# Layer 1's attention in two parts a group: products and copies behind the group's maximum, VectorE's use of them at the group's end, and x added two tiles at a time

## The chip, the cores and the metric

The kernel runs on one core of one Trainium2 chip. The metric is the device time of one execution in microseconds (us), the median of several runs. A separate execution, taken with the hardware profiler, gives the profile and the trace.

## What is computed

The program is a graph network of two layers on 3125 nodes of 256 features, float32 throughout. The part that matters here is the middle of layer 1, which takes the normalised x and adds two things to x: an attention over 50000 edges, and a linear attention over all nodes ("Galerkin").

```python
xn = _layernorm(x)
x = x + _L1_gnn_ref(xn, edge_index, ...) + _L1_mix_ref(xn[None], Wqkv, Wout, bout)[0]

# edges: a message per edge, softmax weights per head, sums per target node
messages = h_fwd[src] * direction[:, 0:1] + h_rev[src] * direction[:, 1:2]
scores = leaky_relu(einsum('ef,hf->eh', messages, attn_forward[0]), 0.2)
exp_scores = exp(scores - scores.max(axis=0))
norm = exp_scores / (segment_sum(exp_scores, dst)[dst] + 1e-10)
out[h] = segment_sum(messages * norm[:, h], dst)

# Galerkin: 8 heads of 64; k and v are normalised over the head
q, k, v = split(xn @ Wqkv.T)
k, v = inst_norm(k), inst_norm(v)
dots = einsum('bhnd,bhne->bhde', k, v)
out = (q @ dots / n) @ Wout.T + bout
```

## The kernel before, in words

`layer0_ffn` ends with 14 adds of x and rows read back from DRAM (L915), two for each of seven chunks of tiles (a tile is 125 nodes; CHUNKS has four of 4 tiles and three of 3). `layer1_mix` then normalises x (`layernorm`, L168 to L185), which leaves the transposed xT, and multiplies each tile by the weights of the edge messages (L191 with wcat). The rows go to a table in DRAM (tab1). Outside the blocks named below, a scheduler decides each engine's order when the program is built.

The loop over edges is written out by hand: in `manual_schedule` the orders of TensorE (PE), VectorE (DVE) and ScalarE (ACT) are those of the program text. The 391 columns of 128 edges are walked in 49 groups of 8. GpSimd (POOL) gathers the rows of a group, three groups ahead, into one of four buffers (`fetch`, L51). A group i then does the following:

- `messages` (L1221 to L1230): DVE forms the messages and the scores of group i and their maximum per partition; PE transposes that (L1232).
- `weigh` (L1278): DVE multiplies the messages of group i - 1 by their weights.
- `maximum` (L1239 to L1241): DVE reduces the transposed maximum, and PE brings the new and the old maximum back to all partitions (L1245).
- `products` (L1286): PE sums the weighted messages of group i - 1 into nodes, with one-hot matrices, in PSUM tiles pw.
- `add` (L1295, L1297): DVE rescales and adds the sums of group i - 2; ACT copies some (L1300, L1302).
- `ones_of` (L1270): DVE builds the one-hot matrices of group i.
- `exponents` (L1250 to L1255): DVE subtracts the maximum, ACT takes Exp.
- `next(todo)`: one step of the generator `galerkin`.

`galerkin` is cut into steps by its `yield`s, and the loop takes one step at the end of each group. Group 0 loads and transposes the weights of k and v (L1456) and takes the mean out of them (L1461 to L1463). Groups 1 to 26 run its loop over 25 tiles: the step first uses tile t - 1 (DVE reduces its squares, L1472, ACT takes Sqrt, L1476, DVE scales v, L1477 and L1478, PE adds to dots, L1480), then makes tile t (PE multiplies xT by the weights, L191, ACT copies the two halves, L1490, and squares them, L1492). Group 27 takes dots out of PSUM and transposes Wout, group 28 forms m2 (L1512, L1513), group 29 forms gm (L1521, L1523). Groups 29 to 35 add the result to x, a chunk each: for each tile PE multiplies xT by gm (L191) into one of the two buffers of the PSUM pool ps_a, and DVE adds it to x (L1529); one more DVE instruction adds bout to the chunk (L1530). Groups 36 to 48 have no step left.

After the loop DVE divides by the sums and adds the edges' result to x. `layer1_ffn` follows and is the same in both kernels.

Of the kernel before, what the change touches and what calls it, by code (L numbers as in the profile page):

```python
# [8 lines left out]
F32 = mybir.dt.float32  # L9
# [79 lines left out]
class Kernel:  # L89
# [1078 lines left out]
    def layer1_mix(self):  # L1168
        nc, tc, a = self.nc, self.tc, self.a
        W, HD = 68, 64  # L1170
        with ExitStack() as m:
# [134 lines left out]
            with tc.manual_schedule(engines={E_.PE, E_.DVE, E_.Activation}):  # L1306
                todo = self.galerkin(big, wk, ps_a, ps_c, xT)
                starts = [(j0, min(GROUP, NJ - j0)) for j0 in range(0, NJ, GROUP)]
                G = len(starts)
                ahead = [fetch(starts[i][0]) for i in range(3)]  # L1310
                msg, exps, summed = {}, {}, {}
                for i in range(G + 2):
                    if i + 3 < G:
                        ahead.append(fetch(starts[i + 3][0]))
                    if i < G:
                        j0, n, g = ahead[i]
                        o, s, pt = messages(j0, n, g)
                    if 0 <= i - 1 < G:
                        weigh(starts[i - 1][1], msg[i - 1][0], exps[i - 1][2])
                    if i < G:  # L1320
                        pb = maximum(pt)
                    if 0 <= i - 1 < G:
                        summed[i - 1] = products(*starts[i - 1], exps[i - 1][2], msg[i - 1][1])
                    if 0 <= i - 2 < G:
                        add(*starts[i - 2], *exps[i - 2][:2], summed[i - 2])
                    if i < G:
                        msg[i] = o, ones_of(j0, n)
                        exps[i] = exponents(n, s, pb)
                    next(todo, None)
                last = exps[G - 1][0]  # L1330
# [112 lines left out]
    def galerkin(self, big, wk, ps_a, ps_c, xT):  # L1443
# [5 lines left out]
        for c4 in range(2):  # L1449
# [3 lines left out]
            for k in range(2):  # L1453
                pt = ps_a.tile([128, 4, 128], F32, name="ln_pt")
                for i in range(4):
                    nc.tensor.transpose(pt[:, i, :], nat[:, i, k * 128:(k + 1) * 128], self.ident)  # L1456
                nc.scalar.copy(wkv[:, k, 512 * c4:512 * c4 + 512],
                               pt.rearrange("p a b -> p (a b)"))
        heads = wkv.rearrange("p k (h c) -> p (k h) c", c=64)
        mean = big.tile([128, 32], F32, name="wkv_mean")  # L1460
        nc.vector.tensor_reduce(mean, heads, AX.X, OP.add)  # L1461
# [4 lines left out]
        pc = ps_c.tile([128, 4, 128], F32, name="pdots")  # L1466
        kvs = {}
        for t in range(NT + 1):
            if t > 0:
                kv, sq = kvs.pop(t - 1)  # L1470
                var = wk.tile([P, 16], F32, name="kv_var")
# [7 lines left out]
                for hp in range(4):  # L1479
# [2 lines left out]
                                     kv[:, 2 * hp:2 * hp + 2, :].rearrange("p a b -> p (a b)"),  # L1482
                                     start=(t == 1 and hp == 0), stop=(t == NT and hp == 3),
                                     skip_group_check=True)
            if t < NT:
                kv = wk.tile([P, 16, 64], F32, name="kv")
                for i in range(2):
                    pk = ps_a.tile([P, 512], F32, name="ln_pt")
                    self.token_matmul(pk, xT, t, wkv[:, :, 512 * i:512 * i + 512])
                    nc.scalar.copy(kv[:, 8 * i:8 * i + 8, :].rearrange("p a b -> p (a b)"), pk)  # L1490
                sq = wk.tile([P, 16, 64], F32, name="kv_sq", bufs=1)
                nc.scalar.activation(sq, kv, AF.Square)  # L1492
                kvs[t] = kv, sq
            yield
        dots = big.tile([128, 4, 128], F32, name="dots")
        nc.vector.memset(dots, 0.0)
        for s in (slice(0, 64), slice(64, 128)):
            nc.vector.tensor_copy(dots[s, :, s], pc[s, :, s])

        woT = big.tile([128, 4, D], F32, name="woT")  # L1500
        nat = wk.tile([128, 2, 512], F32, name="nat4", bufs=1)
        nc.sync.dma_start(nat, a["L1_mix_Wout"].rearrange("(c p) f -> p c f", p=128))
        for cc in range(2):
            pt = ps_a.tile([128, 4, 128], F32, name="ln_pt")
            for i in range(4):
                nc.tensor.transpose(pt[:, i, :], nat[:, cc, i * 128:(i + 1) * 128], self.ident)
            nc.scalar.copy(woT[:, :, cc * 128:(cc + 1) * 128], pt)
        yield
        m2 = big.tile([128, 4, D], F32, name="m2")
        for hp in range(4):  # L1510
            pm = ps_a.tile([128, D], F32, name="ln_pt")
            nc.tensor.matmul(pm, dots[:, hp, :], woT[:, hp, :], start=True, stop=True)  # L1512
            nc.vector.tensor_scalar(m2[:, hp, :], pm, 1.0 / N, None, op0=OP.mult)  # L1513
        wq = wk.tile([128, 4, D], F32, name="nat4", bufs=1)
        nc.sync.dma_start(wq, a["L1_mix_Wqkv"][0:512, :].rearrange("(c p) d -> p c d", p=128))
        yield
        g = big.tile([128, 2, D], F32, name="gm")
        for k in range(2):
            pm = ps_a.tile([128, D], F32, name="ln_pt")
            for hp in range(4):  # L1520
                nc.tensor.matmul(pm, wq[:, hp, k * 128:(k + 1) * 128], m2[:, hp, :],  # L1521
                                 start=(hp == 0), stop=(hp == 3))
            nc.scalar.copy(g[:, k, :], pm)  # L1523
        bout = self.bcast(big, "L1_mix_bout")
        for t0, n in CHUNKS:
            for t in range(t0, t0 + n):
                pm = ps_a.tile([P, D], F32, name="ln_pt")
                self.token_matmul(pm, xT, t, g)
                nc.vector.tensor_add(self.x[:, t, :], self.x[:, t, :], pm)  # L1529
            nc.vector.tensor_add(self.x[:, t0:t0 + n, :], self.x[:, t0:t0 + n, :],  # L1530
                                 bout[:, None, :].to_broadcast([P, n, D]))
            yield


# [393 lines left out]
```

## Time and profile before

| what | value |
|---|---|
| runs shown: median (lowest to highest) | 2810.51 us (2807.82 to 2812.39), 3 runs |
| profiled execution | 3210.01 us, its span 3208.3 us |
| granted TensorE clock, mean over the span | 0.844 |
| busy over the span | PE 2295.1, DVE 1516.4, POOL 1640.0, ACT 539.8 us |
| first gather of the edge loop to the last maximum | 1865.4 to 2515.3 us |

The profile gives times of one execution from the start of its span. A line of the order of time has the start, the duration, the engine, the line of the source, the operation with "output<-inputs", the shapes, a count, and in brackets the idle time of the engine ahead of it with what ended it. "PEld" are PE's weight loads. A float32 matmul shows as two records ("x8" for four matmuls of L191). PEclk is the TensorE clock that was granted, as a share of full speed.

### The profile page before, as it was taken

The numbers are of one execution on the slowest core, as the hardware profiler recorded it, in microseconds if no ns is written. First come the engines' busy times: TensorE is split into PE (matmuls) and PEld (weight loads), VectorE is DVE, ScalarE is ACT, GpSimd is POOL, SyncE is SP. The second block draws the span as 40 slices with busy tenths as digits, with TensorE's granted clock in tenths as the row PEclk, the third lists the DMA queues.
The fourth block names the chain that finished last, engine by engine and source line by source line (L and its number), as shares of the span: only waits on it lengthen the run. The fifth ranks groups of instructions, "written<-read, shape, count | busy, mean of one in ns | idle before, by whom it ended". The sixth has DMA issues, their size and how long they took to land. (4 is left out here: it accounts for less than half of the span.)

```text
span 3208.3 us, 26947 instructions
## 1 busy us (share of the span) xinstructions
PE 2295.1 (72%) x9183; PEld 1705.1 (53%) x9183; DVE 1516.4 (47%) x3630; ACT 539.8 (17%) x1107; POOL 1640.0 (51%) x1490
## 2 busy tenths in 40 slices
PE   1753652169998699899999458798668564788773
PEld 1442431057675466788787345465546353555552
DVE  7874750065547760122111448688569810122225
ACT  1420000000000111222222124344000110122213
POOL 5887887700000170566666157777547246555612
PEclk9865765579998699999999779899878777989886
DMA  8904200034330020655554422221112210111133
GB/s 311 367 2 112 68 12 1 0 78 98 79 98 29 17 76 1 211 169 184 180 177 150 100 69 49 45 48 44 40 31 46 68 37 7 21 33 43 41 90 72
DMA packets 179585, 265.05 MB, mean 83 GB/s; under 512 B 54288, under 2 KB 143866, under 8 KB 176051
## 3 DMA queue, kind: packets, MB, share of 16 engines
q1 hardware_dynamic: 121057, 206.38, 21.1%
q0 software_dynamic: 52480, 47.70, 7.2%
q10 hardware_dynamic: 5894, 9.09, 0.8%
q8 instruction: 76, 1.25, 0.2%
q14 instruction: 78, 0.63, 0.1%
HBM read 178.73 MB, written 84.21 MB: 82 GB/s over the span
## 5 line engine op out<-in xcount | busy, mean ns | idle before, releaser
L51 POOL DMA_INDIRECT g<-tab,t_src x391 | 454.4, 1162 | 259.1 <-issue 111.4
L58 POOL DMA_INDIRECT adj<-ch_sum,ch_place x391 | 488.8, 1250 | 148.0 <-issue 119.4
L460 PE MATMUL psum<-sup,adjT 125*125 125x256 f32 x1250 | 328.2, 411 | 218.6 <-issue 164.5
L460 PEld LDWEIGHTS psum<-sup,adjT 125*125 125x125 f32 x1250 | 250.8, 203 | 285.2 <-issue 200.6
L58 POOL DMA_INDIRECT sorted<-s_rows,pos x256 | 245.9, 961 | 187.6 <-DVE s_rows L1055 119.1
L51 POOL DMA_INDIRECT G<-tabg,g_src x256 | 251.2, 981 | 159.5 <-DVE g_src L1613 83.9
L1286 PE MATMUL pw<-v,hot 128*125 128x260 f32 x1244 | 328.4, 427 | 0.0
L1286 PEld LDWEIGHTS pw<-v,hot 128*125 128x125 f32 x1244 | 259.0, 212 | 50.5
L1644 PE MATMUL fpy<-fw,fh 128*125 128x256 f32 x800 | 208.5, 418 | 86.8 <-ACT fh L1638 36.9
L864 PE MATMUL ph<-xs,w 128*128 128x256 f32 x1024 | 232.3, 385 | 33.4 <-issue 29.6
L1644 PEld LDWEIGHTS fpy<-fw,fh 128*125 128x125 f32 x800 | 164.5, 209 | 135.9 <-ACT fh L1638 43.4
L864 PEld LDWEIGHTS ph<-xs,w 128*128 128x128 f32 x1024 | 194.2, 192 | 71.3 <-issue 44.0
L892 PE MATMUL py<-w,h 128*128 128x256 f32 x1024 | 231.2, 379 | 0.0
L463 DVE TENSOR_TENSOR x<-x,psum 125x512 f32<-125x512 f32 (+1 forms) x104 | 69.1, 666 | 327.2 <-remote 169.4
L1636 PE MATMUL fph<-xT,fw 128*128 128x500 f32 (+1 forms) x448 | 181.2, 553 | 37.0 <-ACT fh L1638 34.0
L892 PEld LDWEIGHTS py<-w,h 128*128 128x128 f32 x1024 | 192.1, 190 | 24.8
L620 POOL MEMSET tier<- 125x64 f32 x1 | 0.2, 157 | 378.1 <-PE psum L460 378.1
L866 ACT ACTIVATE h<-ph,b 128x256 f32<-128x256 f32 x256 | 121.2, 474 | 392.4 <-PE ph L864 357.4
L1030 PE MATMUL pctx<-s_mv,s_ro 128*128 128x256 f32 x512 | 154.9, 413 | 1.9 <-DVE s_mv L1029 1.9
L1636 PEld LDWEIGHTS fph<-xT,fw 128*128 128x128 f32 x448 | 86.2, 195 | 111.8 <-issue 52.8
L170 ACT ACTIVATE ln_rs<-ln_mv,eps 125x4 f32<-125x4 f32 (+1 forms) x28 | 7.5, 296 | 793.0 <-DVE ln_mv L169 793.0
L1638 ACT ACTIVATE fh<-fph,cols 128x500 f32<-128x500 f32 (+1 forms) x112 | 69.5, 633 | 420.4 <-PE fph L1636 226.5
(524 smaller groups left out, 3435.7 us busy)
## 6 DMA issues: line engine op xcount, KB each, us to landing
adjT<-adj SPq DMA_DIRECT2D x25, 1367.2 KB
adj<-zero SPq DMA_DIRECT2D x22, 1536.0 KB
w<-in_L_ffn_W1p_dram SPq DMA_DIRECT2D x32, 1024.0 KB
w<-in_L_ffn_W2p_dram SPq DMA_DIRECT2D x32, 1024.0 KB
slots<-empty SPq DMA_DIRECT2D x1, 8448.0 KB
srow<-slots SPq DMA_DIRECT2D x32, 264.0 KB
adj<-ch_sum,ch_place POOLq DMA_INDIRECT x391
g<-tab,t_src POOLq DMA_INDIRECT x391
```

The lines of the kernel that those rows point to most:

```text
L51: nc.gpsimd.indirect_dma_start(out=out, out_offset=None, in_=table, in_offset=bass.IndirectOffsetOnAxis(ap=idx, axis=0))
L58: return nc.gpsimd.indirect_dma_start(out=table, out_offset=bass.IndirectOffsetOnAxis(ap=idx, axis=0), in_=rows, in_offset=None, **kw)
L460: nc.tensor.matmul(pm[:, i, :], mats[b][:, (a0 + i) * P:(a0 + i + 1) * P], sup[:, b, :], start=(b == b0), stop=(b == b0 + n - 1))
L463: nc.vector.tensor_add(xs, xs, pm[:, :m, :])
L864: nc.tensor.matmul(ph, w1[:, k, f * 128:(f + 1) * 128], xs[:, k, :], start=(k == 0), stop=(k == 1))
L866: nc.scalar.activation(h[:, f, :], ph, AF.Gelu, bias=b1[:, f:f + 1])
L892: nc.tensor.matmul(py, h[:, f, i * 128:(i + 1) * 128], w2[:, f, :], start=(f == 0), stop=(f == FC - 1))
L1030: nc.tensor.matmul(p1, ro[:, f - f0, :], mv, **st)
L1286: nc.tensor.matmul(pw.rearrange("p h c -> p (h c)"), hot[:, i - i0, :], v[:, i, :, :].rearrange("p h c -> p (h c)"), start=(i == i0), stop ...
L1636: nc.tensor.matmul(ph[:, :n * P], w1[:, k, f * 128:(f + 1) * 128], xT[:, k, t0 * P:(t0 + n) * P], start=(k == 0), stop=(k == 1))
L1638: nc.scalar.activation(hs[:, f, :n * P], ph[:, :n * P], AF.Gelu, bias=self.col("L1_ffn_b1", ei * FC + f))
L1644: nc.tensor.matmul(py, hs[:, f, i * P:(i + 1) * P], w2[:, f, :], start=(f == 0), stop=(f == FC - 1))
```

## The change

`galerkin` gets more `yield`s, and each group takes two steps instead of one. The new one stands behind the maximum of the group, ahead of the products of the edges; the old one stays at the end. The first step of a group holds what PE and ACT do for a tile (products, copies, squares), the second what DVE does with the tile before. The transposes of Wout, the products for m2 and gm and the products for x go into first steps, their uses into second ones. Further edits: the squares get two buffers instead of one; Wq is loaded ahead into a buffer of its own; the four products of m2 share two PSUM tiles, the two of gm one; two tiles of x share one PSUM tile and one add; bout is no longer added by VectorE but by a third matmul for each tile, of a row of ones with the row bout, and is loaded as one row. Since `galerkin` now has one step pair more ahead of the chunks, x is added in groups 30 to 36.

The orders of the built programs differ in two further places that the text doesn't touch. On DVE the 14 adds of L915 stood one after the other ahead of layernorm; now layernorm's instructions for a chunk stand between the adds of the next ones, and ACT's square roots and copies of layernorm follow chunk by chunk. On SP the load of Wq stands right behind the first load of the weights of k and v. The order on POOL is the same.

```diff
--- before.py
+++ after.py
@@ -1319,6 +1319,7 @@
                         weigh(starts[i - 1][1], msg[i - 1][0], exps[i - 1][2])
                     if i < G:
                         pb = maximum(pt)
+                    next(todo, None)
                     if 0 <= i - 1 < G:
                         summed[i - 1] = products(*starts[i - 1], exps[i - 1][2], msg[i - 1][1])
                     if 0 <= i - 2 < G:
@@ -1456,6 +1457,7 @@
                     nc.tensor.transpose(pt[:, i, :], nat[:, i, k * 128:(k + 1) * 128], self.ident)
                 nc.scalar.copy(wkv[:, k, 512 * c4:512 * c4 + 512],
                                pt.rearrange("p a b -> p (a b)"))
+        yield
         heads = wkv.rearrange("p k (h c) -> p (k h) c", c=64)
         mean = big.tile([128, 32], F32, name="wkv_mean")
         nc.vector.tensor_reduce(mean, heads, AX.X, OP.add)
@@ -1466,6 +1468,16 @@
         pc = ps_c.tile([128, 4, 128], F32, name="pdots")
         kvs = {}
         for t in range(NT + 1):
+            if t < NT:
+                kv = wk.tile([P, 16, 64], F32, name="kv")
+                for i in range(2):
+                    pk = ps_a.tile([P, 512], F32, name="ln_pt")
+                    self.token_matmul(pk, xT, t, wkv[:, :, 512 * i:512 * i + 512])
+                    nc.scalar.copy(kv[:, 8 * i:8 * i + 8, :].rearrange("p a b -> p (a b)"), pk)
+                sq = wk.tile([P, 16, 64], F32, name="kv_sq")
+                nc.scalar.activation(sq, kv, AF.Square)
+                kvs[t] = kv, sq
+            yield
             if t > 0:
                 kv, sq = kvs.pop(t - 1)
                 var = wk.tile([P, 16], F32, name="kv_var")
@@ -1482,21 +1494,7 @@
                                      kv[:, 2 * hp:2 * hp + 2, :].rearrange("p a b -> p (a b)"),
                                      start=(t == 1 and hp == 0), stop=(t == NT and hp == 3),
                                      skip_group_check=True)
-            if t < NT:
-                kv = wk.tile([P, 16, 64], F32, name="kv")
-                for i in range(2):
-                    pk = ps_a.tile([P, 512], F32, name="ln_pt")
-                    self.token_matmul(pk, xT, t, wkv[:, :, 512 * i:512 * i + 512])
-                    nc.scalar.copy(kv[:, 8 * i:8 * i + 8, :].rearrange("p a b -> p (a b)"), pk)
-                sq = wk.tile([P, 16, 64], F32, name="kv_sq", bufs=1)
-                nc.scalar.activation(sq, kv, AF.Square)
-                kvs[t] = kv, sq
             yield
-        dots = big.tile([128, 4, 128], F32, name="dots")
-        nc.vector.memset(dots, 0.0)
-        for s in (slice(0, 64), slice(64, 128)):
-            nc.vector.tensor_copy(dots[s, :, s], pc[s, :, s])
-
         woT = big.tile([128, 4, D], F32, name="woT")
         nat = wk.tile([128, 2, 512], F32, name="nat4", bufs=1)
         nc.sync.dma_start(nat, a["L1_mix_Wout"].rearrange("(c p) f -> p c f", p=128))
@@ -1505,30 +1503,51 @@
             for i in range(4):
                 nc.tensor.transpose(pt[:, i, :], nat[:, cc, i * 128:(i + 1) * 128], self.ident)
             nc.scalar.copy(woT[:, :, cc * 128:(cc + 1) * 128], pt)
+        wq = wk.tile([128, 4, D], F32, name="nat4b", bufs=1)
+        nc.sync.dma_start(wq, a["L1_mix_Wqkv"][0:512, :].rearrange("(c p) d -> p c d", p=128))
+        yield
+        dots = big.tile([128, 4, 128], F32, name="dots")
+        nc.vector.memset(dots, 0.0)
+        for s in (slice(0, 64), slice(64, 128)):
+            nc.vector.tensor_copy(dots[s, :, s], pc[s, :, s])
         yield
         m2 = big.tile([128, 4, D], F32, name="m2")
-        for hp in range(4):
-            pm = ps_a.tile([128, D], F32, name="ln_pt")
-            nc.tensor.matmul(pm, dots[:, hp, :], woT[:, hp, :], start=True, stop=True)
-            nc.vector.tensor_scalar(m2[:, hp, :], pm, 1.0 / N, None, op0=OP.mult)
-        wq = wk.tile([128, 4, D], F32, name="nat4", bufs=1)
-        nc.sync.dma_start(wq, a["L1_mix_Wqkv"][0:512, :].rearrange("(c p) d -> p c d", p=128))
+        pms = []
+        for i in range(2):
+            pm = ps_a.tile([128, 2, D], F32, name="ln_pt")
+            for hp in range(2):
+                nc.tensor.matmul(pm[:, hp, :], dots[:, 2 * i + hp, :], woT[:, 2 * i + hp, :], start=True, stop=True)
+            pms.append(pm)
+        yield
+        for i, pm in enumerate(pms):
+            nc.vector.tensor_scalar(m2[:, 2 * i:2 * i + 2, :], pm, 1.0 / N, None, op0=OP.mult)
         yield
         g = big.tile([128, 2, D], F32, name="gm")
+        bout = big.tile([1, D], F32, name="bout")
+        nc.sync.dma_start(bout, a["L1_mix_bout"][None, :])
+        pm = ps_a.tile([128, 2, D], F32, name="ln_pt")
         for k in range(2):
-            pm = ps_a.tile([128, D], F32, name="ln_pt")
             for hp in range(4):
-                nc.tensor.matmul(pm, wq[:, hp, k * 128:(k + 1) * 128], m2[:, hp, :],
+                nc.tensor.matmul(pm[:, k, :], wq[:, hp, k * 128:(k + 1) * 128], m2[:, hp, :],
                                  start=(hp == 0), stop=(hp == 3))
-            nc.scalar.copy(g[:, k, :], pm)
-        bout = self.bcast(big, "L1_mix_bout")
+        nc.scalar.copy(g, pm)
+        yield
+        yield
         for t0, n in CHUNKS:
-            for t in range(t0, t0 + n):
-                pm = ps_a.tile([P, D], F32, name="ln_pt")
-                self.token_matmul(pm, xT, t, g)
-                nc.vector.tensor_add(self.x[:, t, :], self.x[:, t, :], pm)
-            nc.vector.tensor_add(self.x[:, t0:t0 + n, :], self.x[:, t0:t0 + n, :],
-                                 bout[:, None, :].to_broadcast([P, n, D]))
+            pms = []
+            for t1 in range(t0, t0 + n, 2):
+                m = min(2, t0 + n - t1)
+                pm = ps_a.tile([P, 2, D], F32, name="ln_pt")
+                for i in range(m):
+                    for k in range(2):
+                        nc.tensor.matmul(pm[:, i, :], xT[:, k, (t1 + i) * P:(t1 + i + 1) * P], g[:, k, :],
+                                         start=(k == 0), stop=False)
+                    nc.tensor.matmul(pm[:, i, :], self.full[0:1, :P], bout, start=False, stop=True)
+                pms.append((t1, m, pm))
+            yield
+            for t1, m, pm in pms:
+                xs = self.x[:, t1:t1 + m, :]
+                nc.vector.tensor_add(xs, xs, pm[:, :m, :])
             yield
 
 
```

## The prediction

> **What bounds the kernel now.** I read the stretches first, then the order of time in one group, engine by engine, then the waits. Layer 1's attention walks 49 groups of edges, and a group's length is the distance between two maxima on VectorE (L1239). In groups 2 to 26 galerkin adds one tile of tokens to each group, in 29 to 35 it adds the product to x, in 36 to 48 nothing. In the stretches PE and DVE, both, are filled while the tiles run, and neither while x is added; PEclk falls with it (columns: stretch, length, busy us of PE, PEld, DVE, ACT, POOL with instructions, PEclk, DMA share, GB/s).
>
> ```profile
> 1910.00:1985.00 75.00, 68.84 (x286) 47.39 (x285) 67.15 (x133) 34.82 (x57) 59.46 (x52) 1.00 0.22 48
> ...
> 2255.00:2405.00 150.00, 99.65 (x361) 78.14 (x362) 87.93 (x169) 5.08 (x26) 73.09 (x67) 0.81 0.14 31
> ```
>
> The maxima stand 11.28 to 14.14 us apart in the 20 tile groups that nothing unexplained stretches (mean 12.1); in five others DVE waits 2.9 to 11.5 us for something the trace doesn't show. One tile group, VectorE, then PE, then ScalarE, in order of time:
>
> ```profile
> 1933.00 0.28 DVE L1239 TENSOR_REDUCE top<-psm 4x1 f32<-4x128 f32 x1 [0.16 <-PE psm L1232]
> ...
> 1939.15 0.20 DVE L1477 RECIPROCAL kv_both<-kv_both 125x8 f32<-125x8 f32 x1 [0.37 <-ACT kv_both L1476]
> 1939.39 0.69 DVE L1478 TENSOR_TENSOR kv<-kv,kv_both 125x512 f32<-125x512 f32 x1
> 1940.11 0.72 DVE L1221 TENSOR_TENSOR msg<-g,t_dir 128x544 f32<-128x544 f32 x1
> ...
> 1942.62 2.30 DVE L1278 TENSOR_TENSOR v<-msg,v 128x2048 f32<-128x2048 f32 x1
> 1944.93 0.28 DVE L1239 TENSOR_REDUCE top<-psm 4x1 f32<-4x128 f32 x1
> ```
>
> ```profile
> 1929.25 3.60 PE L191 MATMUL ln_pt<-wkv,xT 128*125 128x512 f32 x8
> ...
> 1933.51 0.40 PE L1245 MATMUL psm<-ident,top 4*128 4x4 f32 x2 [0.55 <-DVE top L1240]
> 1933.84 6.40 PE L1286 MATMUL pw<-v,hot 128*125 128x260 f32 x28
> ```
>
> ```profile
> 1931.17 0.59 ACT L1490 COPY kv<-ln_pt 125x512 f32<-125x512 f32 x1 [3.99 <-issue]
> 1932.89 0.59 ACT L1490 COPY kv<-ln_pt 125x512 f32<-125x512 f32 x1 [1.13 <-PE ln_pt L191]
> 1933.51 1.06 ACT L1492 ACTIVATE kv_sq<-kv 125x1024 f32<-125x1024 f32 x1
> 1934.47 0.18 ACT L1302 COPY unit<-top_b 125x4 f32<-125x4 f32 x1
> 1934.66 1.28 ACT L1253 ACT_TABLE_LOAD   x1
> 1937.27 0.26 ACT L1253 ACTIVATE v<-score 128x32 f32<-128x32 f32 x1 [1.33 <-DVE score L1251]
> 1937.41 0.19 ACT L1255 ACTIVATE grown<-top_b 128x4 f32<-128x4 f32 x1
> 1937.62 1.28 ACT L1476 ACT_TABLE_LOAD   x1
> 1938.91 0.21 ACT L1476 ACTIVATE kv_both<-kv_both 125x8 f32<-125x8 f32 x1
> ```
>
> To see: the products of k and v (L191) run before the maximum, so copies, square and the first table load are over 1.33 us before Exp can start, and DVE waits only 0.37 for the square root. DVE and PE close the loop almost together (0.16).
>
> Where x is added, DVE waited 7.11 us for the products behind the group's pw, then 0.44 at each further tile, because two PSUM buffers hold one tile each; all waits of L1529 for L191 are 41.7 us.
>
> ```profile
> 2304.41 0.42 DVE L1529 TENSOR_TENSOR x<-x,ln_pt 125x256 f32<-125x256 f32 x1 [7.11 <-PE ln_pt L191]
> ```
>
> Last, the clock: the same 26 records of pw took 8.66 us after PE had mostly idled for 3.3 us (2456.64 to 2459.95, a 0.27 us transpose within), 5.96 when it had not.
>
> ```profile
> 2460.33 8.66 PE L1286 MATMUL pw<-v,hot 128*125 128x260 f32 x26
> ...
> 2469.98 5.96 PE L1286 MATMUL pw<-v,hot 128*125 128x260 f32 x26
> ```
>
> **What the Trainium skill says.** "TensorE: Matmul & The Clock Gate", the table of specifications at its head: ScalarE and VectorE take their queues strictly in order, and PE may only pull weight loads ahead of matmuls. The trace agrees: in no group does a matmul of L191 or L1286 pass L1245 while that waits. The same page, "Part 1: The HAM clock gate": half clock after an idle window of about 3.4 us, full clock after a busy one. The trace agrees with 8.66 against 5.96. "ScalarE: Activation LUTs", "What ACT_TABLE_LOAD costs": exp and sqrt lie in different sets, a switch is a load of about 1.28 us plus a drain of about 1.38. The trace has the 1.28, twice a group, but no such drain: in the group of 2234.77 Exp starts 1.37 after its load starts.
>
> **The change, part by part.** Names of before; the compiled order of after shows where each instruction stands.
>
> *Tile groups, first half.* PE's order becomes L1232, L1245, L191, pw, L1480; ScalarE's becomes copy, copy, Square, the copy of acc or unit, load, Exp, grown, load, Sqrt; VectorE's stays. L191 now stands behind L1245, which waits for the maximum; behind L191 wait the copies, and behind those, on ScalarE, the Sqrt of the tile before, for which DVE waits at L1477 ahead of the next group. That is a closed loop of queues. With the maximum at 0 and gaps from the lines above: L191 starts at 0.84 (1933.84 - 1933.00); second copy 3.64 later, 4.48; Square 0.62 later, 5.10; unit copy 6.06; load 6.25; Exp 1.37 later, 7.62; load 7.97; Sqrt 1.29 later, 9.26; L1477 9.50; L1478 9.74; the next L1221 at 10.45; L1278 2.51 later, 12.95; the next maximum 2.20 later (2311.10 to 2313.30), **15.15**. DVE alone would have reached L1477 at about 5.8, so it idles some 3.7 us a group. The wait for psm (0.16 to about 1.1) goes; the wait for Sqrt is what is late next. 24 groups have both halves: 24 x (15.15 - 12.1) = **+73 us** at full clock.
>
> *The clock.* In this loop PE has pw done at 0.84 + 3.60 + 6 = 10.4, L1480 from 10.6 to 11.7, then only L1232 until the next L1245 at 15.7: 4 us idle but for 0.3, more than the 3.3 that brought the half clock above. I take it that L191, on the loop, then starts at half clock. Bounds per group: nothing, or 1.7 to 2.7 (7.65 and 8.66 against 5.96). I take 2.0: a loop of 17.15, 24 x 5.05 = **+121 us**.
>
> *Adding x, woT, m2, gm.* Before, the ten groups from 27 take 168.8 us (2243.56 to 2412.38). After, x is due in groups 30 to 36. PE per group: 0.84 to the first product; three matmuls a tile (the third brings bout), 6 records of 0.226 (3.62 / 16), so 5.4 for four tiles, 4.1 for three; pw of 13 on average, 26 x 0.229 = 5.95; 0.3 to the next maximum. So 12.5, or 11.2: DVE's own chain is 11.8, hence about 12.5 and 11.8, 85 for the seven with no idle stretch in PE, plus 2 for a slow first. DVE's 25 adds of 0.42 and 7 of 0.96 to 1.22 become 14 (a 512-wide one I estimate at 0.69, between 0.42 for 256 and 0.72 for 544); they start when PE is at pw. The groups of woT, m2 and gm have no long wait left: 10.6, 10.6, 9.5. Sum 118, **-51 us**. Bounds: -40 if PE keeps half clock for a window a group, -60 if the groups fall near the bare 9.3.
>
> *Compiled order ahead of the stage.* DVE's layernorm (L168 to L178) now stands between the adds of L915 instead of after all 14. Before, the adds wait for their loads (13.9 us in sum) from 1798.80 to 1824.2, and layernorm ends at 1844.8. DVE's work is 8 x 1.23 + 6 x 0.96 for the adds and some 19.3 of layernorm's 20.6; interleaved, with the 0.9 that the second add waits, it ends near 1834.6. PE's and ScalarE's work on it, the table and the first gather follow: **-10 us**, at worst 0.
>
> *Costing nothing.* The load of wq goes to its own buffer and SP issues it near 1819, where SP is idle until 1849.66; bout's load shrinks to one row. POOL's order is the same, and its gathers (at most 11.7 us for eight) fit in every length above but the last groups', unchanged. The second kv_sq buffer lets Square run before the reduce of the tile before. 25 matmuls for bout (11 us of PE) lie in the sums above.
>
> **Sum.** 121 - 51 - 10 = +60 us. The profiled execution took 3210.0 us (span 3208.3, 1.7 around it), 399.5 over the median of 2810.5; its waits for nothing shown (169.4, 117.1, 58.9, 39.7 us on the largest rows) are nearly that gap, so I carry differences in us to the median and leave those waits out. 3270 profiled, **2870** as median.
>
> **Rivals.** (1) PE stays at full clock: for it, one gap of 2.0 us in group 27 did no harm; against it, 4 us is longer than the 3.3 that did. 73 - 61 = +12: 2822. (2) Faster: the loop doesn't close on ScalarE, because PE starts L191 without waiting for L1245, or copies come sooner. Place: PE's queue at L1245. Then tile groups stay near 12.1 and the rest is kept: 2750. It decides below a loop of 12.1 + 61/24 = 14.6, half a us under my full-clock walk. Against it speaks the order on three engines. (3) x isn't quicker because PE at half clock is the bound: +75, 2885.
>
> **How the numbers follow.** Half clock in the loop 0.50, full clock 0.23, faster 0.18, x not quicker 0.09. About 0.2% (5.6 us) is what a measurement here can tell from no change. Faster 0.18; same 0.07, the lower edge of rival 1; slower 0.75. The range goes from 2790, which takes in a loop of 14 us at full clock, to 2900, a loop of 17.9 with half of the gain at x lost; mostly the deeper part of rival 2 is left out. The slower cases alone span 2815 to 2900.
>
> **What would show it.** Maxima of tile groups 15 to 18 us apart; a wait of several us at the reciprocal for ScalarE's kv_both; Exp starting after its score has long been ready; the first records of L191 at about 0.85 us instead of 0.43 (both spacings are in the group of 2228.05); groups of x at 12 to 13 us with PE filled; the first gather 10 us earlier after the adds of L915. I am wrong if the reciprocal waits under 1 us or the maxima stay at 12.

## The result and the profile after

| what | before | after |
|---|---|---|
| median (lowest to highest) | 2809.16 us (2806.57 to 2812.39), 4 runs | 2869.68 us (2866.86 to 2870.82), 4 runs |
| ratio, 95% interval | | 1.022 [1.0206, 1.0234] |
| profiled execution, its span | 3210.0, 3208.3 us | 2866.86, 2865.1 us |
| granted TensorE clock over the span | 0.844 | 0.876 |

The change makes the kernel 60.5 us slower. The spans of the two profiled executions can't be set against each other: in some series of runs PE stands still again and again for something the profile doesn't show, and an execution is some 360 to 400 us longer. The kernel before took 3210 us beside experiments 1, 2, 3 and 7, 3174 beside 4, 5 and 6, and 2808 to 2810 beside the rest; the number of the chip doesn't decide it, since chip 4 gave 3174 and, half an hour later, 2808. So totals are compared with the kernel before of the same series only, and traces by the lengths of stretches. The ratios leave out runs that took over 1.5% more than the fastest of the same kernel.

**Where the time went.** A group's length is again the distance between two maxima (L1239). Lines L1470 and later have other numbers after the change: the copies of k and v are L1476, the square root L1488, the reciprocal L1489, the scaling of v L1490, the products for x L1543 and L1545, the add to x L1550.

| stretch | predicted | measured before, after | difference |
|---|---|---|---|
| tile groups, 24 from maximum 2 to 26 | +121 | 24 x 12.1 = 290.4 (the 20 undisturbed ones' mean), 405.6 | +115 |
| ten groups from maximum 27 to 37 | -51 | 168.8, 124.9 | -44 |
| first add of L915 to first gather | -10 | 66.6, 59.4 | -7 |
| sum | +60 | | +64, median +60.5 |

First the stretches view of the kernel after, over most of its tile groups (stretch, length, busy us of PE, PEld, DVE, ACT, POOL with instructions, PEclk, DMA share, GB/s):

```profile
1690.00:2060.00 370.00, 281.05 (x982) 181.86 (x980) 234.12 (x463) 122.64 (x201) 206.60 (x188) 0.85 0.14 36
```

In a stretch of undisturbed tile groups of before PE was busy for 68.84 of 75 us (92%) and DVE for 67.15 (90%), at a clock of 1.00. Now PE is busy for 76% and DVE for 63%, and the clock is 0.85. No engine is full, and yet the groups are longer: a loop through several queues sets the pace, as the experiments below show. Here is the order of time in one tile group of the kernel after (engines mixed):

```profile
1857.39 0.27 DVE L1239 TENSOR_REDUCE top<-psm 4x1 f32<-4x128 f32 x1
...
1857.90 0.45 PE L1245 MATMUL psm<-ident,top 4*128 4x4 f32 x2 [2.21 <-DVE top L1240]
...
1858.28 5.78 PE L191 MATMUL ln_pt<-wkv,xT 128*125 128x512 f32 x8
...
1862.09 0.58 ACT L1476 COPY kv<-ln_pt 125x512 f32<-125x512 f32 x1 [10.27 <-PE ln_pt L191]
...
1863.89 6.74 PE L1286 MATMUL pw<-v,hot 128*125 128x260 f32 x30
1864.09 0.59 ACT L1476 COPY kv<-ln_pt 125x512 f32<-125x512 f32 x1 [1.42 <-PE ln_pt L191]
1864.71 1.06 ACT L1478 ACTIVATE kv_sq<-kv 125x1024 f32<-125x1024 f32 x1
1865.67 0.18 ACT L1302 COPY unit<-top_b 125x4 f32<-125x4 f32 x1
1865.87 1.28 ACT L1253 ACT_TABLE_LOAD   x1
1867.16 0.26 ACT L1253 ACTIVATE v<-score 128x32 f32<-128x32 f32 x1
...
1867.50 1.28 ACT L1488 ACT_TABLE_LOAD   x1
1868.80 0.21 ACT L1488 ACTIVATE kv_both<-kv_both 125x8 f32<-125x8 f32 x1
1869.04 0.20 DVE L1489 RECIPROCAL kv_both<-kv_both 125x8 f32<-125x8 f32 x1 [6.11 <-ACT kv_both L1488]
...
1869.88 0.72 DVE L1221 TENSOR_TENSOR msg<-g,t_dir 128x544 f32<-128x544 f32 x1
1870.46 1.06 PE L1492 MATMUL pdots<-kv 125*128 125x128 f32 x8
...
1872.61 0.27 PE L1232 MATMUL psm<-ident,mx 128*4 128x128 f32 x1 [1.09 <-DVE mx L1230]
1874.58 0.27 DVE L1239 TENSOR_REDUCE top<-psm 4x1 f32<-4x128 f32 x1
```

Read it as one round: maximum, PE's L1245, the eight records of L191, two copies, Square, two table loads with their functions, the reciprocal, and only then the next messages and the next maximum, 17.19 us later. The scores that Exp takes were ready at 1861.38, and Exp starts at 1867.16: the table load wasn't late because of its data but because it stands behind the copies. From 1871.52 PE has nothing but one transpose of 0.27 us until 1875.09, and it had a gap like that ahead of 1857.90 too. The granted clock is 0.50 from 1855.67 to 1862.50: the first records of this L191 start 0.85 us and more apart, its last ones 0.43, and the eight take 5.78 us. The waits of VectorE over the same stretch (what, for whom, us in sum, times, longest):

```profile
DVE kv_both L1489 <- ACT kv_both L1488: 138.2, 24, 6.3
```

That is the row of the reciprocal, which before waited for ACT 21 times, 7.6 us in all and at most 0.4. The first group with x, after the change:

```profile
2122.34 1.13 PE L1543 MATMUL ln_pt<-gm,xT 128*125 128x256 f32 x4
...
2123.40 0.69 PE L1545 MATMUL ln_pt<-bout,full 1*125 1x256 f32 x2
...
2124.02 1.13 PE L1543 MATMUL ln_pt<-gm,xT 128*125 128x256 f32 x4
...
2126.06 0.68 DVE L1550 TENSOR_TENSOR x<-x,ln_pt 125x512 f32<-125x512 f32 x1
...
2129.06 5.09 PE L1286 MATMUL pw<-v,hot 128*125 128x260 f32 x22
2129.17 0.69 DVE L1550 TENSOR_TENSOR x<-x,ln_pt 125x512 f32<-125x512 f32 x1 [2.43 <-PE ln_pt L1545]
```

The 512-wide add takes the 0.68 to 0.69 that the prediction had estimated, but VectorE still waits for PE at the second: a tile takes PE 2124.02 - 2122.34 = 1.68 us. These waits come to 16.9 us (11 times), where before had 41.7. In the seven groups of x PE is busy for 87.2 of 91.5 us and VectorE for 66.9.

### The profile page after: what moved, and what is told of

It is laid out like the page before. It is cut to its first block, busy times and chain, and to the rows that moved or that the text cites. A ratio compares the mean times of both kernels' runs of the same rounds, so it can differ in the third digit from the quotient of the medians.

```text
span 2865.1 us, 27019 instructions
## 1 busy us (share of the span) xinstructions
PE 2263.3 (79%) x9233; PEld 1685.6 (59%) x9233; DVE 1504.9 (53%) x3610; ACT 539.8 (19%) x1106; POOL 1657.0 (58%) x1490
## 5 line engine op out<-in xcount | busy, mean ns | idle before, releaser
L58 POOL DMA_INDIRECT adj<-ch_sum,ch_place x391 | 512.4, 1310 | 149.1 <-issue 112.2
L460 PE MATMUL psum<-sup,adjT 125*125 125x256 f32 x1250 | 292.3, 393 | 50.5 <-DMA adjT<-adj 39.5
L1286 PE MATMUL pw<-v,hot 128*125 128x260 f32 x1244 | 295.8, 397 | 0.0
L460 PEld LDWEIGHTS psum<-sup,adjT 125*125 125x125 f32 x1250 | 240.9, 195 | 91.8 <-DMA adjT<-adj 37.3
L1286 PEld LDWEIGHTS pw<-v,hot 128*125 128x125 f32 x1244 | 241.1, 195 | 55.1 <-issue 14.4
L1663 PE MATMUL fpy<-fw,fh 128*125 128x256 f32 x800 | 187.0, 390 | 33.9 <-DVE y L1665 29.0
L1663 PEld LDWEIGHTS fpy<-fw,fh 128*125 128x125 f32 x800 | 152.9, 193 | 71.9 <-DVE y L1665 30.6
L866 ACT ACTIVATE h<-ph,b 128x256 f32<-128x256 f32 x256 | 121.1, 473 | 367.9 <-PE ph L864 335.3
L191 PE MATMUL ln_pt<-wkv,xT 128*125 128x512 f32 x200 | 137.1, 849 | 0.0
L895 DVE TENSOR_SCALAR yo<-py,own 128x256 f32<-128x256 f32 x64 | 29.6, 481 | 193.1 <-PE py L892 193.1
L58 POOL DMA_INDIRECT slots<-rows,abi x50 | 72.5, 1449 | 99.0 <-DVE r_cum L944 84.1
```

Source lines behind the costliest of these rows:

```text
L58: return nc.gpsimd.indirect_dma_start(out=table, out_offset=bass.IndirectOffsetOnAxis(ap=idx, axis=0), in_=rows, in_offset=None, **kw)
L191: self.nc.tensor.matmul(out, xT[:, k, t * P:(t + 1) * P], w[:, k, :], start=(k == 0), stop=(k == 1))
L460: nc.tensor.matmul(pm[:, i, :], mats[b][:, (a0 + i) * P:(a0 + i + 1) * P], sup[:, b, :], start=(b == b0), stop=(b == b0 + n - 1))
L866: nc.scalar.activation(h[:, f, :], ph, AF.Gelu, bias=b1[:, f:f + 1])
L1286: nc.tensor.matmul(pw.rearrange("p h c -> p (h c)"), hot[:, i - i0, :], v[:, i, :, :].rearrange("p h c -> p (h c)"), start=(i == i0), stop ...
L1663: nc.tensor.matmul(py, hs[:, f, i * P:(i + 1) * P], w2[:, f, :], start=(f == 0), stop=(f == FC - 1))
```

## The experiments

The theory: the tile groups got longer because the split closes a loop PE, ACT, DVE, in which L191 waits for the maximum and the copies push both table loads behind themselves (15.15 us at full clock), and because PE, idle in that loop, falls to half clock at L191 (2 more). The rivals: the clock alone; another cost of the split (buffers, steps, the added `yield`s); PE without half clock.

**1. The first step ahead of the maximum.** Only PE's wait goes: L191 stands ahead of L1245.

```diff
@@ the kernel after
+                    next(todo, None)
                     if i < G:
                         pb = maximum(pt)
-                    next(todo, None)
```

> The changed kernel with one line moved: the group's first step stands ahead of the maximum instead of behind it, so that PE's L191 no longer stands behind L1245. Theory (a closed loop: maximum, L1245, L191, copies, Square, Exp, Sqrt on ScalarE, scaling of v, next maximum): L191 starts right behind L1232, 1.8 us ahead of the maximum, Sqrt is done 6.9 after it, tile groups are 12.6 us long instead of 16.9, PE stays at full clock: 24 x 4.3 = 103 us less than the changed kernel, 2767. Rival (two steps a group, or the new buffers, are slow wherever the step stands): tile groups stay near 17, 2870. Rival (PE at half clock is the bound whatever the order): 15 or more, 2825.

Measured: ratio to before 0.9883 [0.9817, 0.9949]. The tile groups from 9 to 26 are 11.56 to 14.20 us long, mean 12.7, with PE, ACT and DVE doing the same work as after. VectorE's waits at the reciprocal in this run, from 1950 to 2260 us (what, for whom, us in sum, times, longest; "issue" is nothing that the profile shows):

```profile
DVE kv_both L1489 <- ACT kv_both L1488: 15.0, 12, 2.8
DVE kv_both L1489 <- issue: 14.0, 9, 2.8
```

The place of that one step accounts for nearly the whole loss; the split as such costs some 0.6 us a group.

**2. The tiles back in the second step,** all else as after.

```diff
@@ galerkin, the kernel after
         for t in range(NT + 1):
-            if t < NT:
-                kv = wk.tile([P, 16, 64], F32, name="kv")
...
             yield
             if t > 0:
...
+            if t < NT:
+                kv = wk.tile([P, 16, 64], F32, name="kv")
...
             yield
```

> The changed kernel with the tile's products, copies and Square put back behind the use of the tile before, in the group's second step; all that concerns x stays changed. Theory: tile groups go back to the 12.1 of before while x keeps its gain of 44 us and the table its 7: 2870 - 24 x 4.8 = 2755, that is 55 under the kernel before. Rival (the gain at x is only moved time, given back in the groups after it because the gathers are then late): 2809.

Measured: 0.9826 [0.9748, 0.9904], which is 31 to 81 us under the before beside it; tile groups at 11.3 to 14.2 where nothing unexplained stretches them. Run again, beside the versions at the end and without the unexplained stretches:

> Once more the kernel after with products, copies and Square of a tile put back into the second step, behind the use of the tile before, so that it is compared on the same chip with the two versions of this call. Theory: tile groups 12.1, the ten groups 125, the table -7: 51 us less than the kernel before.

Measured: 2768.67 us, 0.9848 [0.983, 0.9866], 41 less than the 2809.53 of before. The 24 tile intervals sum to 291.3 (12.1 each) and the ten groups to 125.1, both as expected; but the last eleven groups take 112.8 instead of 101.3 in the kernel after. The 10 us that are missing are there, and experiment 8 says why.

**3. No square root.** The reciprocal takes the product of the variances directly, so ACT loads no second table.

```diff
@@ galerkin, the kernel after
-                nc.scalar.activation(both, both, AF.Sqrt)
```

> The changed kernel without the square root of the product of the variances (the factor is 1 over the product), so ScalarE has no Sqrt and no table load in the tile groups. Theory: with nothing of ScalarE behind the copies that VectorE waits for, VectorE's chain is 11.5 us and PE's queue 12.0: tile groups of 12.0, 2870 - 24 x 4.9 = 2752. Rival (PE's own queue at half clock sets the length): still 15 to 17 us, 2825 to 2870.

Measured: 0.9916 [0.9876, 0.9955]; the tile groups from 14 to 26 are 11.11 to 14.29 us, mean 12.5 where 12.0 was expected. Without ACT's two loads and Sqrt in it the round no longer sets the pace: PE's wait for the maximum does nearly no harm. The edit removes both loads and DVE's wait for ACT at once, so it doesn't price either alone.

**4. PE kept busy.** Two matmuls that nothing reads are put into PE's idle stretch ahead of the maximum's transpose (L1232), and two behind it.

```diff
@@ layer1_mix, the kernel after
+                def fill(i, k):
+                    if 2 <= i <= 25:
+                        idle = ps_a.tile([P, 512], F32, name="ln_pt")
+                        for _ in range(k):
+                            nc.tensor.matmul(idle, xT[:, 0, :P], xT[:, 1, :512], start=True, stop=True)
...
+                    fill(i, 2)
                     if i < G:
                         pb = maximum(pt)
...
                     next(todo, None)
+                    fill(i, 2)
```

> The kernel after, and in groups 2 to 25 two matmuls nothing reads (128x512 by a 128-row square of xT, four records, about 1.6 us at full clock) ahead of the maximum's PE part and two more behind the group's last PE instruction, so that PE isn't left with a small transpose alone for some 4 us a group. They compute nothing that is used. Theory (the 17 us of a tile group are a loop of 15.15 on ScalarE and the half clock at the products of k and v, about 1.9 a group): products of k and v back from 5.8 to about 3.6 to 4.0 us, tile groups 15.2 to 15.5 us, 40 us less than the kernel after. Rival A (the half clock isn't on the loop; something else makes 17): groups stay at 17, or 18 to 20 with the added 3.2 us of PE. Rival B (the clock alone makes the loss): groups near 12.6.

The kernel after, run beside it, is the yardstick here:

> The kernel after, unchanged, on the same chip as the other runs of this call, so that they can be compared with it directly. Every theory: tile groups 16.9 us, ten groups from the end of the tiles 125 us, 1.02 times the kernel before where the chip runs the kernel before in about 2810 us.

Measured: e5_warm 1.0101 [1.0066, 1.0135] to before, e8_after_again 1.0237 [1.0208, 1.0265]; the difference of 0.0136 is 43 us of 3174.21. From group 10 on, tile groups are 14.96 to 15.46 us with the added matmuls and 16.67 to 17.47 without. One group of e5_warm:

```profile
2180.81 1.88 PE L1317 MATMUL ln_pt<-xT 128*125 128x512 f32 x4
...
2182.64 1.88 PE L1317 MATMUL ln_pt<-xT 128*125 128x512 f32 x4
2184.38 0.27 DVE L1239 TENSOR_REDUCE top<-psm 4x1 f32<-4x128 f32 x1
...
2185.21 3.70 PE L191 MATMUL ln_pt<-wkv,xT 128*125 128x512 f32 x8
...
2193.89 0.20 DVE L1498 RECIPROCAL kv_both<-kv_both 125x8 f32<-125x8 f32 x1 [3.99 <-ACT kv_both L1497]
```

and its stretch of tile groups:

```profile
2060.00:2260.00 200.00, 187.76 (x698) 116.82 (x697) 142.29 (x280) 71.67 (x118) 114.67 (x106) 1.00 0.16 37
```

With 3.8 us more of PE work in it, a group is 1.9 us shorter: the clock is 1.00, L191 is 3.70 instead of 5.78, and DVE waits 3.99 instead of 6.11. Rival A asked for 17 us and more, rival B for 12.6; neither came. What stays is the loop at full clock. So the loss of 115 us splits into 24 x (15.15 - 12.1) = 73 for the loop and the remaining 42 for the clock.

**5. The split alone,** with x tile by tile and bout on VectorE as before.

```diff
@@ layer1_mix and galerkin, the kernel before, with the tile loop of the kernel after
                         pb = maximum(pt)
+                    next(todo, None)
...
         for t in range(NT + 1):
+            if t < NT:
+                kv = wk.tile([P, 16, 64], F32, name="kv")
...
+            yield
             if t > 0:
...
+        yield
         dots = big.tile([128, 4, 128], F32, name="dots")
```

> The split tile loop of the kernel after, with the part behind it (transposes of Wout, m2, gm, x tile by tile, bout added by VectorE) as before, in second steps. Theory (three separate terms): tile groups 16.9 us on average, the ten groups from the end of the tiles 165 to 170 us as before (the kernel after has 125), so about 44 us more than the kernel after and 108 us more than the kernel before. Rival (the split of the tiles and x share a cause, such as the clock or the buffers): the ten groups below 140, or the tile groups at another length than 16.9.

Measured: 1.0389 [1.0359, 1.0419] to before, and 48 us more than the kernel after beside it (44 expected). Against before that is 114 to 133 us, more than the 108 expected; the kernel after, too, loses more here than in the result (2.4% instead of 2.2%), and why isn't known. Its tile groups sum to 422.48 us, those of the kernel after beside it to 422.47 (in both, two groups of 24 to 25.4 us that nothing explains); its ten groups take 169.05 (before 168.8). The two terms don't touch each other.

**6. No matmul for bout,** so that bout is left out of x.

```diff
@@ galerkin, the kernel after
                         nc.tensor.matmul(pm[:, i, :], xT[:, k, (t1 + i) * P:(t1 + i + 1) * P], g[:, k, :],
-                                         start=(k == 0), stop=False)
-                    nc.tensor.matmul(pm[:, i, :], self.full[0:1, :P], bout, start=False, stop=True)
+                                         start=(k == 0), stop=(k == 1))
```

> The kernel after without the third matmul of each tile of x, so that bout is left out of x; everything else as after. Theory (in the groups of x PE is the bound and each of the 25 one-row matmuls for bout costs 0.69 us and a gap of about 0.3, against the 0.45 of the prediction): the seven groups of x, 12.97 us on average in the kernel after, become 11.8 to 12.0, where VectorE's own chain of 11.8 is the bound; 7 us less in all. Rival (the matmuls for bout lie in PE's idle time and the wait of VectorE has another cause, such as the clock after an idle stretch): the groups stay at 12.6 to 13.2, no change of time.

Measured: the ten groups take 106.8 us where the kernel after beside it has 125.1, and the seven of x (31 to 37) sum to 73.4 instead of 91.6. That is 18.3 us for 25 matmuls, 0.73 each: PE was the bound. The expectation's 11.8, where VectorE's chain was to take over, falls: the groups are 9.97 to 11.28. Part of the gain is lost again: the last eleven groups take 114.2 us instead of 101.2, some of it in one group of 16.1 that nothing explains, some as experiment 8 says. The time itself (3222 to 3294 us in four runs, in a series that stretches PE) says nothing on 18 us. What is left of VectorE's waits in those groups:

```profile
DVE top L1239 <- PE psm L1232: 6.1, 4, 2.7
DVE x L1549 <- PE ln_pt L1543: 1.3, 2, 0.7
```

Nor is it the matmul for bout alone that costs. In the kernel after a record of gm inside its run of four starts 0.216 us behind the one before it. At each change between gm (128 rows) and bout (one row) the last record ahead of it and the first behind it take 0.30 to 0.32, in all 25 tiles. Without bout the records of gm go on at 0.216 from tile to tile. (The expectation's 0.69 us with a gap of 0.3 was too much for a matmul for bout itself: from start to start its two records take 0.62.)

**7. Before, with an unused tile.** The tile and its one-column memset are all that is added; the scheduler then puts layernorm between the adds of L915, as in the kernel after.

```diff
@@ layer1_mix, the kernel before
+            pad = big.tile([128, 2048], F32, name="pad")
+            nc.vector.memset(pad[:, 0:1], 0.0)
             xT = big.tile([128, 2, N], F32, name="xT2")
```

> The kernel before with one tile of 8 KB a partition that only a one-column memset touches. The built order then has layernorm between the adds of L915, as in the changed kernel, and the rest as before. Theory (the earlier table of the changed kernel comes from addresses alone): from the first L915 to the first gather 59.4 us instead of 66.6, 7 us less in all, 2802. Rival (the gain is lost again because the gathers wait later): 2809.

Measured: 0.9953 [0.9931, 0.9975], 15 us less with 8 to 22 in the interval, where 7 were expected. From the lines of L915 (duration least/median/most in ns, first and last start) and of the gathers, before:

```profile
L915 DVE TENSOR_TENSOR x<-x,w x14: 957/1224/1227, 1798.8 to 1823.2; 125x1024 f32<-125x1024 f32 x8, 125x768 f32<-125x768 f32 x6
```

```profile
L51 POOL DMA_INDIRECT g<-tab,t_src x391: 942/947/2486, 1865.4 to 2507.3; - x196
```

and before with the unused tile:

```profile
L915 DVE TENSOR_TENSOR x<-x,w x14: 924/1206/1226, 1857.5 to 1891.4; 125x1024 f32<-125x1024 f32 x8, 125x768 f32<-125x768 f32 x6
```

```profile
L51 POOL DMA_INDIRECT g<-tab,t_src x391: 939/947/2507, 1916.2 to 2548.3; - x196
```

From the first add to the first gather it is 66.6 us, and 58.7 with the tile (59.4 in the kernel after): 7 to 8 us come from the order, and nothing in `galerkin` is needed for it. Not every change of the tiles brings it: experiment 5, which gives the squares their second buffer, has 65.9 us and the last run of experiment 8 has 66.8. What the time gained beyond those 8 us, if anything, isn't shown. This run also holds an undisturbed tile loop of before, 290.7 us for the 24 intervals, which is the 24 x 12.1 of the table.

**8. Better versions, and what stops them.** Both add bout to x ahead of the edge loop, in place of the 25 matmuls; one has the tiles in the second step (experiment 2), the other the first step ahead of the maximum (experiment 1).

```diff
@@ layer1_mix, added to experiments 2 and 1; the matmul for bout is taken out as in 6
                 todo = self.galerkin(big, wk, ps_a, ps_c, xT)
+                bout = self.bcast(big, "L1_mix_bout")
+                for t0, n in CHUNKS:
+                    nc.vector.tensor_add(self.x[:, t0:t0 + n, :], self.x[:, t0:t0 + n, :],
+                                         bout[:, None, :].to_broadcast([P, n, D]))
```

> The version with the old place for the tiles (products, copies and Square in the second step, behind their use), x two tiles at a time in two steps, and bout added to x by seven adds of VectorE (0.96 to 1.22 us each, 8 us in sum) ahead of the edge loop, where VectorE waits for the first gather, in place of the 25 matmuls. Theory: tile groups as before (12.1), the ten groups from the end of the tiles 107 us as without bout against 168.8 before (-62), the table -7, the seven adds hidden: 69 us less than the kernel before, some 18 us less than the same version with the matmuls for bout. Rival (the seven adds aren't hidden and delay the first messages): 61 less.

> The kernel after with the first step ahead of the group's maximum instead of behind it, and bout added to x by VectorE ahead of the edge loop as in the other version of this call. Theory: tile groups 12.6 (+12 on the 24 intervals), the ten groups from the end of the tiles 105 to 110, the table -7: 55 us less than the kernel before. Rival (ahead of the maximum the products for x delay it, so that VectorE idles in every group of x): the ten groups at 115 or more, 45 less than before or a smaller gain.

Measured, with before at 2809.53 us on the same chip: e9_best_late 2763.29, 0.9834 [0.982, 0.9848]; e10_best_ahead 2762.17, 0.9835 [0.9822, 0.9849]. Both beat both kernels, but not by what was expected (46 us instead of 69, and 47 instead of 55). The groups say where it went: e9_best_late has its tile groups at 12.1 and its ten groups at 110.1 us (expected 107), e10_best_ahead 12.7 and 96.8 (better than the 105 to 110 expected). The seven adds aren't wholly hidden: from the first add of L915 to the first gather it is 62.8 and 62.6 us instead of 59.4. And the last eleven groups, 101.3 in the kernel after, take 122.3 and 121.1, each some 11.1 instead of 9.2. In them VectorE waits for gathered rows (first fence, e9_best_late), and POOL issues without a pause (second):

```profile
DVE msg L1221 <- DMA g<-tab,t_src: 28.1, 12, 2.8
```

```profile
2132.12 0.94 POOL L51 DMA_INDIRECT g<-tab,t_src  x1 [0.30 <-issue]
2133.37 0.94 POOL L51 DMA_INDIRECT g<-tab,t_src  x1 [0.30 <-issue]
2134.62 0.94 POOL L51 DMA_INDIRECT g<-tab,t_src  x1 [0.30 <-issue]
...
2140.93 1.89 POOL L51 DMA_INDIRECT g<-tab,t_src  x1 [0.30 <-issue]
```

In these two and in the second run of experiment 2, POOL has no pause but those 0.30 us from the first gather to the last. The kernel after could go faster at the end because its long tile groups had let POOL run ahead: by the maximum of group 37 it had started the gathers of 3.4 groups more than were used, e9_best_late those of 0.6.

In the groups view of the kernel after the 391 gathers take 446 us (1.14 each), and with the gaps of 0.30 behind them (117) that makes 563. From the first to the last maximum these versions take 563.7 and 561.5 us, experiment 2 570.7, the kernel after 672.9. The last run puts that floor to the test:

```diff
@@ layer1_mix, the kernel after
-                todo = self.galerkin(big, wk, ps_a, ps_c, xT)
+                todo = iter(())
```

> The kernel after without the generator's steps: the whole linear attention (k, v, dots, Wout, bout and its part of x) is left out, and the loop over edges is all that is left of this stage. Theory (the 391 gathers on GpSimd, 1.14 us each with a gap of 0.30 after it, 1.44 x 391 = 563 us, are a floor under the edge loop whatever the other engines do): the groups are 11.3 to 11.7 us long from the third on, VectorE waits 2 to 3 us a group for gathered rows, and the first to the last maximum is 545 to 565 us, hardly shorter than the 561 to 571 of the versions with the attention; the kernel is at 2745 to 2765 us where the kernel before takes 2810. Rival (the groups of 11.3 at the end of the faster versions come from something else, such as the clock or a transfer beside them): groups near 9.2 us, 440 us for the loop, 2640 us.

Measured: 2748.57 us, 0.9788 [0.9772, 0.9804], with before at 2807.79. With the whole linear attention left out the groups are still 10.35 to 12.10 us long from the second on, and from the first to the last maximum it is 542.6 us. That is a little under the range expected, since the gathers themselves are quicker here: one starts every 1.41 us, where it is 1.46 to 1.48 in the versions with the attention. VectorE waits for rows 47 times:

```profile
DVE msg L1221 <- DMA g<-tab,t_src: 121.0, 47, 4.6
```

So the gathers, issued one after the other, are a floor under the edge loop. Leaving the attention out altogether is worth only some 14 us more than moving its pieces to where they don't wait (19 in the loop, less some 4 ahead of it, where this run has 66.8 us).

## Why the prediction was right, point by point

- **The loop.** Predicted round at full clock 15.15 us; with the clock kept full by experiment 4 the groups are 15.06 and 15.24 in turn. Experiments 1 and 3 open the round at PE and at ACT, and the groups fall to 12.7 and 12.5. This step is shown.
- **The clock.** 2.0 us a group were taken, with a reason (some 4 us of idle PE but for a transpose); measured are 1.9 (17.05 against 15.15), with L191 at 5.78 us against 3.70 and its first records 0.85 us apart, as the prediction had asked for. Rival 1, full clock and 2822, falls. The loop with half clock was put at 17.15; the steady groups are 16.93 and 17.19 in turn. The term came to +115 and not +121 because 24 groups are 0.1 us shorter than that and the first one takes 13.82 us.
- **Points of the walk.** From the maximum: second copy 6.70 (4.48 at full clock, predicted, and 2 for the clock), Exp 9.77 (7.62), Sqrt 11.41 (9.26), reciprocal 11.65 (9.50), messages 12.49 (10.45), maximum 17.19 (15.15). After the 2.2 at the copies no further difference builds up.
- **x: the mis-sized term.** -44 instead of -51. The step "6 records of 0.226, so 5.4 for four tiles" is where it was off: 0.226 a record holds inside a run of gm (0.216), but each tile now has two changes between 128 rows and one, and the four records at them take some 0.1 us more each. So a tile takes PE 1.68 us instead of 1.36. Put into the prediction's own sum, that gives groups of 13.8 us for four tiles and 12.1 for three; measured are 13.8 and 12.1 on average, 91.5 for the seven instead of 87.4. The other 2.8 us lie in the three groups of woT, m2 and gm, 33.5 instead of 30.7, and aren't explained. "DVE's own chain is 11.8" was too long as well; without bout the groups go down to 9.97.
- **The order ahead of the stage.** -7.2 instead of -10. VectorE ends layernorm 37.9 us after the first add of L915, where 35.8 was predicted and before had 46.0; at the first gather 7.2 of these 8.1 us are left. Experiment 7 shows that an unused tile brings it as well; it isn't earned by the parts of the change that it was made for.
- **Rivals.** Rival 2 put "faster" at 2750 us and let it decide below 14.6 us a group. Its mechanism is real: experiments 1 and 2 have PE's order otherwise and are faster than before. Its price was wrong: of the 61 us, the second run of experiment 2 has 41. Some 10 are lost at x and in the order, as in the kernel after, and 10 in the last eleven groups, because POOL's gathers, which "fit in every length above", don't fit in shorter ones. 2762 is the least that a whole kernel reached here. Rival 3 (x not quicker) falls by 44 us; its price of +75 holds only for a smaller gain at x, since with none the prediction's sum is 121 - 10 = +111. The upper end of the range, 2900, is too low for what it names as well: a loop of 17.9 us with half the gain at x comes to 2914.
- **The gap of 399.5 us** between the profiled execution of before and its median was rightly left out of the sum, but it isn't a property of being profiled: two series of runs show it in all their executions, and the profiled run of after doesn't. What PE waits for in it stays open.

The mechanism was right, but that the median came out within 1 us of 2870 is luck: the three terms are off by -6, +7 and +3 us, and what lies outside them by some -3. Why the sum of the three, +64, is above the +60.5 isn't settled; the last eleven groups, 101.3 against 102.9, give back 1.6 of it.

## What to carry to other kernels

Before an instruction is moved behind a wait on one engine, walk once round all the queues that feed back to that wait, at the durations of the trace, and take the length of the round, not the busy time of any engine, as the new pace. Look in the walk for an engine that gets a few idle us: if it is PE, the matmuls after the gap may run at half clock, as they did here after 3.6 us with one transpose in them, and where they are part of the round that is paid each time. And before a gain is priced, find what runs at its own pace beside the work (here 391 gathers, one every 1.41 to 1.48 us): no rearrangement of the other engines' work got the loop below that.

## What the runs showed of the hardware

- Four matmuls a group that no one reads, 3.8 us of PE, shortened the group from 17.05 to 15.15 us; the granted clock over these groups was 1.00 with them and 0.85 without.
- A float32 matmul over one row by 256 columns isn't cheaper than one over 128 rows, and changing between the two costs: records over 128 rows start 0.216 us apart in a run, and at each change the last ahead of it and the first behind it take 0.30 to 0.32. Leaving out the 25 of one row saved 0.73 us each.
- GpSimd's 391 gathers with nothing to hold them up started one every 1.41 us: 1.10 each and 0.30 between them.
- An 8 KB tile per partition that nothing uses changed the compiled order: 58.7 us instead of 66.6 from the first add to the first gather, and 8 to 22 us off the kernel before.
- The Trainium skill, "ScalarE: Activation LUTs", "What ACT_TABLE_LOAD costs", adds a drain of about 1.38 us to each load. The tile groups of the kernel after agree with the load (1.28) and not with the drain: Exp starts at 1867.16, 1.29 after its load does, and Sqrt at 1868.80, 1.30 after its own, and either load starts within 0.02 us of the end of the instruction ahead of it.
- The same kernel took 2808 to 2810, 3174 or 3210 us in different series of runs; chip 4 gave both 3174 and 2808.
